# A recurrence in front of an attention kernel: order of the input chunks' normalization, and the refinements of the roots spread over steps

## The chip, the cores and the metric

The kernel runs on one core of a Trainium2 chip, in float32. The metric is the device time of one execution in microseconds (us); less is better. The engines named below are the tensor engine (PE, with its weight loads shown apart as PEld), the vector engine (DVE), the scalar engine (ACT), the general engine (POOL) and the queue engine that issues most transfers (SP). Each engine works through its own instructions in order, and waits on the others by semaphores.

## The reference

A layer of a small sequence model, over x of shape (2, 2048, 256): a plain recurrence with a residual, then a sparse-expert attention with a residual. Both read x through a layer norm.

```python
def _layernorm(x, axis=-1, eps=1e-05):
    m = jnp.mean(x, axis=axis, keepdims=True)
    v = jnp.var(x, axis=axis, keepdims=True)
    return (x - m) / jnp.sqrt(v + eps)
...
xi = jnp.einsum('btd,hd->bth', x, Wi) + bi
def step(h, xt):
    h_new = jnp.tanh(xt + h @ Wh.T + bh)
    return (h_new, h_new)
...
x = L0_attn_x
x = x + _L0_attn_ref(_layernorm(x, axis=-1), Wi, bi, Wh, bh)
x = x + _L0_ffn_ref(_layernorm(x, axis=-1), Wq, Wk, Ws, Wd, Wv, Wo)
```

The attention part has 8 heads of 64, 5 experts of which each token and head takes 2, and is not touched by the change, but for the roots of its own layer norm.

## The kernel before

**Chunks.** Time is cut into 128 segments of 16 steps, for both batches. Chunk c (c = 0 to 15) holds step c of all 128 segments: a tile of 128 partitions by 2 batches by 256. All segments advance together, so one step of the recurrence is one small product for 128 segments.

**Front, pass a (lines 325 to 338).** A loop over k works as a hand-written software pipeline. The order of the calls is the order of the instructions in each engine's queue. In iteration k, it calls in this order:

- turn_in(k-1): four PE transposes of the normalized chunk (line 271), and one DVE copy to SBUF (275);
- project_in(k-2): eight PE matmuls with Wi (283), and two ACT copies with the bias to xi (290);
- step_a(k-3), from k = 5 on: for each batch 8 PE matmuls with Wh (300), a DVE add (308) and an ACT tanh (309);
- norm_in(k): the normalization of chunk k, batch 0 on ACT (248) and batch 1 on POOL (256);
- measure(k+4): for each batch DVE statistics (122) and their aggregate (123). At the last chunk of a group this also makes the group's 1/sqrt(var + eps): three integer and scalar operations (131, 133, 135), then four refinements of three DVE instructions each (141, 143, 145), then the offset -mean times root (152).

The groups of input chunks are IN = [(0, 2), (2, 2), (4, 4), (8, 4), (12, 4)], given as (first chunk, count). Before the loop, measure(0) to measure(3) run, and the bias sum (327). Pass a starts at step 2 and gives the end state of each segment; those ends, moved by one segment, are the starts of pass b.

**Front, pass b (lines 408 to 422).** A second hand-written loop, over k = 0 to 18: step_b(k) runs the step again from the right starts, residual(k-1) turns the state back (four PE transposes, line 347), adds it to x on DVE (348), writes x1 to DRAM from SP's queue (351) and takes the statistics of batch 0 (122, 123). At the last chunk of a group of OUT = [(0, 8), (8, 4), (12, 4)] the roots are computed at once, as above. norm(c) then normalizes chunk c of batch 0 (ACT 379, POOL or DVE 384), and turn(c), an iteration later and only for c below 12, transposes it (392) and copies it (393) into xT, which the attention reads. Chunks 0 and 1 are normalized at k = 9, and so on, two an iteration; chunks 8 to 11 at k = 13 and 14, chunks 12 to 15 at k = 17 and 18. compare() ends the pass: it checks that the end states of both passes agree, else a slow exact version runs at the end (lines 968 and on).

**Attention.** It begins with keys (line 469), queries (486) and experts (511) of the first head on PE; its first keys need xT of chunks 0 to 7 and the PSUM that the front used. Its own layer norm for batch 1 takes the same roots(), with the operations put two per window at windows 21 and on (lines 749 and 866).

**Buffers.** The normalized chunks rotate over three SBUF buffers, the transposes' and the projection's PSUM tiles over two each, the step's PSUM has one per batch.

Of the kernel before, what the change touches and what calls it, by code (L numbers as in the profile page):

```python
# [8 lines left out]
F32 = mybir.dt.float32  # L9
# [5 lines left out]
P = 128  # L15
# [5 lines left out]
def rnn_then_switchhead_kernel(  # L21
# [17 lines left out]
    E, _, DH = Wv.shape  # L39
    H = Wq.shape[1] // DH  # L40
    KC = D // P
    NCH = T // P
# [82 lines left out]
    def roots(pool, var, n, nm):  # L125

        got = {}

        def begin():
            v = pool.tile([P, n], F32, tag="rt_v", name=f"v{nm}")  # L130
            nc.vector.tensor_scalar(v, var, EPS, None, ALU.add)
            half = pool.tile([P, n], I32, tag="rt_i", name=f"i{nm}")
            nc.vector.tensor_scalar(half, v.bitcast(I32), 1, None, ALU.logical_shift_right)
            y = pool.tile([P, n], I32, tag="rt_y", name=f"y{nm}")
            nc.vector.tensor_scalar(y, half, -1.0, float(0x5F3759DF), ALU.mult, ALU.add)
            got["v"], got["y"] = v, y.bitcast(F32)

        def better(k):
            v, y = got["v"], got["y"]
            a = pool.tile([P, n], F32, tag="rt_a", name=f"a{nm}_{k}")  # L140
            nc.vector.scalar_tensor_tensor(a, y, -0.5, y, ALU.mult, ALU.mult)
            h = pool.tile([P, n], F32, tag="rt_h", name=f"h{nm}_{k}")
            nc.vector.tensor_tensor(h, a, v, ALU.mult)
            z = pool.tile([P, n], F32, tag="rt_z" if k < 3 else "rt_r", name=f"z{nm}_{k}")
            nc.vector.scalar_tensor_tensor(z, h, 1.5, y, ALU.add, ALU.mult)
            got["y"] = z

        return got, [begin] + [lambda k=k: better(k) for k in range(4)]

    def offset(dst, mean, root):  # L150

        nc.vector.scalar_tensor_tensor(dst, mean, -1.0, root, ALU.mult, ALU.mult)  # L152
# [53 lines left out]
    TOL = 4 * 2.0**-23  # L206
    S0 = 2
    apart = const.tile([P, 1], F32, name="apart")
    IN = [(0, 2), (2, 2), (4, 4), (8, 4), (12, 4)]
    OUT = [(0, 8), (8, 4), (12, 4)]  # L210
    LATE = 12
    late_of = {}
    with tc.tile_pool(name="prep", bufs=2) as pp, tc.tile_pool(
        name="lna", bufs=2
    ) as lnp, tc.tile_pool(name="step", bufs=2) as sp, tc.tile_pool(
        name="ps_f", bufs=2, space=PSUM
    ) as ps_f, tc.tile_pool(name="ps_h", bufs=1, space=PSUM) as ps_h, tc.manual_schedule():
        group_in = {c: g for g, (c0, n) in enumerate(IN) for c in range(c0, c0 + n)}
        group_out = {c: g for g, (c0, n) in enumerate(OUT) for c in range(c0, c0 + n)}
        norm_of, made, h_of = {}, {}, {}  # L220

        def measure(c):
            g = group_in[c]
            c0, n = IN[g]
            if c == c0:
                norm_of[g] = [lnp.tile([P, 4, B, 2], F32, tag="mv", name=f"mva{g}")]
            mv = norm_of[g][0]
            for b in range(B):
                st = lnp.tile([P, 6], F32, tag="st", name=f"sta{c}_{b}")
                stats((st, mv[:, c - c0, b, :]), xt[c][:, b, :])  # L230
            if c < c0 + n - 1:
                return
            mvf = mv[:, 0:n].rearrange("p j b t -> p (j b) t")
            got, ops = roots(lnp, mvf[:, :, 1], n * B, f"a{g}")
            for f in ops:
                f()
            nb = lnp.tile([P, n * B], F32, tag="nb", name=f"nba{g}")
            offset(nb, mvf[:, :, 0], got["y"])
            norm_of[g] += [got["y"], nb]

        def norm_in(c):
            g = group_in[c]
            _, r, nb = norm_of[g]
            xn = pp.tile([P, B, D], F32, tag="xn", bufs=3, name=f"xn{c}")
            for b in range(B):
                k = (c - IN[g][0]) * B + b
                if b == 0:
                    nc.scalar.activation(
                        xn[:, b, :],
                        xt[c][:, b, :],  # L250
                        AF.Identity,
                        scale=r[:, k : k + 1],
                        bias=nb[:, k : k + 1],
                    )
                else:
                    nc.gpsimd.tensor_scalar(  # L256
                        xn[:, b, :],
                        xt[c][:, b, :],
                        r[:, k : k + 1],
                        nb[:, k : k + 1],  # L260
                        ALU.mult,
                        ALU.add,
                    )
            made[c] = xn

        def turn_in(c):
            xn = made.pop(c)
            tp = ps_f.tile([P, KC, B, P], F32, tag="tp", name=f"tpa{c}")
            for kc in range(KC):
                for b in range(B):  # L270
                    nc.tensor.transpose(
                        tp[:, kc, b, :], xn[:, b, kc * P : (kc + 1) * P], ident
                    )
            xnT = pp.tile([P, KC, B, P], F32, tag="xnT", name=f"xnT{c}")
            nc.vector.tensor_copy(xnT, tp)
            made["T", c] = xnT

        def project_in(c):
            xnT = made.pop(("T", c))
            for mc in range(KC):  # L280
                px = ps_f.tile([P, B, P], F32, tag="px", name=f"px{c}_{mc}")
                for kc in range(KC):
                    nc.tensor.matmul(
                        px.rearrange("p b n -> p (b n)"),
                        lhsT=wi[:, kc, mc * P : (mc + 1) * P],
                        rhs=xnT[:, kc].rearrange("p b n -> p (b n)"),
                        start=kc == 0,
                        stop=kc == KC - 1,
                    )
                nc.scalar.activation(  # L290
                    xi[:, mc, c], px, AF.Identity, bias=bsum[:, mc : mc + 1]
                )
# [27 lines left out]
        def step_b(s):  # L320
            for b in range(B):
                prev = ends[:, :, b, 0:NS] if s == 0 else hs[:, :, s - 1, b, :]
                advance("b", s, b, prev, hs[:, :, s, b, :])

        for c in range(4):
            measure(c)
        nc.vector.tensor_tensor(bsum, bias[:, 0, :], bias[:, 1, :], ALU.add)
        for k in range(NCH + 3):
            if 0 <= k - 1 < NCH:
                turn_in(k - 1)  # L330
            if 0 <= k - 2 < NCH:
                project_in(k - 2)
            if S0 <= k - 3:
                step_a(k - 3)
            if k < NCH:
                norm_in(k)
            if k + 4 < NCH:
                measure(k + 4)

        mv2 = lnp.tile([P, NCH, 2], F32, tag="mv2", bufs=1, name="mv2")  # L340
        root_of = {}

        def residual(c):
            tp = ps_f.tile([P, B, KC, P], F32, tag="tp", name=f"tpb{c}")
            for b in range(B):
                for kc in range(KC):
                    nc.tensor.transpose(tp[:, b, kc, :], hs[:, kc, c, b, :], ident)
            nc.vector.tensor_tensor(
                xt[c], xt[c], tp.rearrange("p b c d -> p b (c d)"), ALU.add
            )  # L350
            nc.sync.dma_start(out=x1d[c], in_=xt[c])
            st = lnp.tile([P, 6], F32, tag="st2", name=f"stb{c}")
            stats((st, mv2[:, c, :]), xt[c][:, 0, :])
            g = group_out[c]
            c0, n = OUT[g]
            if c < c0 + n - 1:
                return
            m = mv2[:, c0 : c0 + n, :]
            got, ops = roots(lnp, m[:, :, 1], n, f"b{g}")
            for f in ops:  # L360
                f()
            nb = lnp.tile([P, n], F32, tag="nb2", name=f"nbb{g}")
            offset(nb, m[:, :, 0], got["y"])
            root_of[g] = (got["y"], nb)

        def norm(c):
            g = group_out[c]
# [39 lines left out]

        jobs = {}
        for c in range(NCH):
            k = 9 + c // 2 if c < 8 else max(OUT[group_out[c]][0] + OUT[group_out[c]][1] + 1, 9 + c // 2)  # L410
            k += (c % 2) if c >= 12 else 0
            jobs.setdefault(k, []).append((norm, c))
            if c < LATE:
                jobs.setdefault(k + 1, []).append((turn, c))
        for k in range(max(jobs) + 1):
            if k < S:
                step_b(k)
            if 1 <= k <= S:
                residual(k - 1)
            for f, c in jobs.get(k, []):  # L420
                f(c)
# [481 lines left out]
    with tc.manual_schedule():  # L903
# [7 lines left out]
        b, n = heads[units[last][0]][0], units[last][1]  # L911
        NW = NT // RUN
        for W in range(NW + LAG):
# [20 lines left out]
            for t in old:  # L934
                if t // HC == last:
                    c = t % HC
# [32 lines left out]
    with tc.If(flag > 0):  # L969
        with tc.tile_pool(name="fr", bufs=1) as fr, tc.tile_pool(  # L970
            name="f2", bufs=2
# [86 lines left out]
            for k in range(2):  # L1058
                for b in range(B):
                    new_logits(b, k)  # L1060
                    for c in range(k * HN, (k + 1) * HN):
# [14 lines left out]
                        got, ops = roots(f2, mv[:, :, 1], 1, f"fb{b}_{c}")  # L1076
# [36 lines left out]
        with tc.tile_pool(name="rows", bufs=1) as rows, tc.tile_pool(  # L1113
            name="row2", bufs=2
        ) as row2, tc.tile_pool(name="ps_a", bufs=1, space=PSUM) as ps_a, tc.tile_pool(
            name="ps_b", bufs=2, space=PSUM
# [150 lines left out]
```

## Time and profile before

| what | us |
|---|---|
| median of 3 runs | 1447.45 (1447.43 to 1448.62) |
| the profiled execution's own time | 1448.96 |
| its span, first to last instruction | 1447.2 |

The span by stages, from the start of one to the start of the next (PE instructions' starts), with the busy time of the engines in it:

| stage | from, to | length | PE | DVE | ACT | mean granted PE clock |
|---|---|---|---|---|---|---|
| pass a, until the transposes of k = 6 | 0 to 33.06 | 33.06 | 12.88 | 21.99 | 8.71 | 1.00 |
| pass a, k = 6 to 15 | 33.06 to 89.95 | 56.89 | 41.69 | 26.38 | 22.80 | 1.00 |
| pass a, k = 16 to 18 | 89.95 to 99.94 | 9.99 | 9.74 | 2.90 | 3.91 | 1.00 |
| pass b, steps 0 to 8 | 99.94 to 121.00 | 21.06 | 20.91 | 15.84 | 7.51 | 1.00 |
| pass b, steps 9 and 10 | 121.00 to 130.85 | 9.85 | 6.79 | 7.15 | 2.50 | 0.83 |
| pass b, steps 11 and 12 | 130.85 to 136.28 | 5.43 | 5.43 | 3.65 | 3.45 | 1.00 |
| pass b, step 13 | 136.28 to 141.82 | 5.54 | 2.83 | 4.85 | 1.92 | 1.00 |
| pass b, steps 14, 15 and its end | 141.82 to 149.05 | 7.23 | 6.19 | 5.85 | 4.55 | 1.00 |
| attention | 149.05 to 1447.20 | 1298.15 | | | | 0.73 to 1.00 |

PE is busy for 1340.4 us of the span (93%), DVE for 1141.6, POOL for 1009.5 and ACT for 705.0. A matmul's end is modelled in this profile, so starts are read rather than ends. An idle time in brackets behind a line of the timeline is that of the engine just ahead of the instruction, with what released it.

### The profile page before, as it was taken

Reading aid. Unit: us, or ns where it says so; the run is one execution under the profiler, and the core shown is the slowest. Engines: PE = TensorE matmul, PEld = TensorE weight load, DVE = VectorE, ACT = ScalarE, POOL = GpSimd, SP = SyncE. Lnnn points to the kernel's source line nnn. Section 1 sums busy time; section 2 is a strip of 40 time slices with the busy share of each in tenths; the row PEclk is TensorE's granted clock in tenths of the full one; section 3 lists DMA queues with packets and bytes.
Section 4 is the critical chain, followed back from the end, with each engine's and each line's share of the span. In section 5 each row is a group of like instructions: output and inputs, shape, how many; then the busy total and the mean of one; then the engine's idle time right before and its main releaser. Section 6 shows DMA issues by size and latency. Waiting matters only on the chain.

```text
span 1447.2 us, 36443 instructions
## 1 busy us (share of the span) xinstructions
PE 1340.4 (93%) x15450; PEld 635.1 (44%) x15450; DVE 1141.6 (79%) x2131; ACT 705.0 (49%) x911; POOL 1009.5 (70%) x590
## 2 busy tenths in 40 slices
PE   4788779999989999989999999999999999999986
PEld 3678324444334444433344455444444444444444
DVE  6537668989887687889988877888888888888752
ACT  2433325555445555544455444555555555555451
POOL 1100038888878768768888866888888888888960
PEclk9999979999999999999999999999999999999999
DMA  6002115657665666556667556566666666766643
GB/s 189 1 9 87 66 45 136 176 149 156 129 144 129 151 147 148 132 103 145 132 139 174 134 136 152 140 139 145 141 145 139 139 143 137 157 139 146 140 106 102
DMA packets 66314, 186.99 MB, mean 129 GB/s; under 512 B 8928, under 2 KB 26464, under 8 KB 66144
## 3 DMA queue, kind: packets, MB, share of 16 engines
q0 software_dynamic: 25056, 97.53, 36.4%
q1 hardware_dynamic: 39456, 86.46, 18.8%
q8 instruction: 123, 2.02, 0.5%
q10 hardware_dynamic: 1632, 0.61, 0.2%
q14 instruction: 47, 0.39, 0.1%
HBM read 59.79 MB, written 50.33 MB: 76 GB/s over the span
## 4 chain that ended last, share of the span: by engine, by line
PE 58%; issue 15%; DVE 11%; POOL 3%; ACT 1%; DVEq 0%; POOLq 0%; ACTq 0%
PE o L629 28%; PE s L570 12%; DVE p L586 7%; PE pq L486 4%; PE pk L469 4%; PE pz L806 3%; PE pv L511 2%; PE pc L648 2%; PE pc L661 1%; PE pl L597 1%; POOL es L613 1%; POOL es L609 1%; POOL es L619 1%; PE py L790 1%; DVE gates L200 0%
## 5 line engine op out<-in xcount | busy, mean ns | idle before, releaser
L586 DVE TENSOR_SCALAR_CACHE_REDUCE p<-s 128x1024 f32<-128x1024 f32 x512 | 596.4, 1221 | 114.2 <-PE s L570 112.1
L602 ACT ACTIVATE p<-p,low 128x1024 f32<-128x1024 f32 x512 | 546.1, 1140 | 55.3 <-DVE low L599 54.9
L570 PE MATMUL s<-q,k 64*32 64x512 f32 x4096 | 482.6, 603 | 13.7 <-DVE p L586 10.4
L570 PE MATMUL s<-qs,k 64*32 64x512 f32 x4096 | 482.6, 603 | 11.1 <-DVE p L586 5.9
L629 PE MATMUL o<-p,v 128*64 128x256 f32 x4096 | 472.5, 383 | 0.0
L609 POOL TENSOR_TENSOR es<-p,p 128x1024 f32<-128x1024 f32 x126 | 329.3, 2613 | 164.9 <-ACT p L602 164.9
L629 PEld LDWEIGHTS o<-p,v 128*64 128x64 f32 x4096 | 282.7, 137 | 194.7 <-ACT p L602 48.6
L613 POOL TENSOR_TENSOR es<-es,p 128x1024 f32<-128x1024 f32 x126 | 299.9, 2380 | 9.9
L640 ACT COPY os<-o 128x256 f32<-128x256 f32 x64 | 23.8, 372 | 394.2 <-PE o L629 394.2
L570 PEld LDWEIGHTS s<-qs,k 64*32 64x32 f32 x4096 | 120.8, 107 | 147.7 <-issue 75.6
L570 PEld LDWEIGHTS s<-q,k 64*32 64x32 f32 x4096 | 120.7, 107 | 147.0 <-issue 67.6
L619 POOL TENSOR_TENSOR es<-es,es 128x1024 f32<-128x1024 f32 x63 | 151.4, 2403 | 4.0 <-DMA es<-p 3.9
L615 POOL DMA_DIRECT2D es<-p x126 | 109.9, 873 | 19.1 <-POOL es L613 14.9
L555 DVE TENSOR_TENSOR pr<-xq,pw 128x1280 f32<-128x1280 f32 x60 | 89.3, 1488 | 31.3 <-ACT pw L539 31.3
L704 DVE TENSOR_TENSOR pro<-pc,mr 128x1280 f32<-128x1280 f32 (+1 forms) x65 | 95.6, 1471 | 2.2
L560 DVE TENSOR_REDUCE v<-pr 128x256 f32<-128x1280 f32 x64 | 94.9, 1486 | 2.1
L620 POOL TENSOR_TENSOR es<-es 128x512 f32<-128x512 f32 x63 | 85.5, 1357 | 4.9
L469 PE MATMUL pk<-xT,wk 128*32 128x512 f32 x512 | 62.2, 604 | 2.5 <-ACT xT L393 1.0
L486 PE MATMUL pq<-xT,wq 128*32 128x512 f32 x512 | 62.2, 603 | 1.4
L720 POOL DMA_DIRECT2D yd<-pro x48 | 56.6, 1180 | 0.8 <-DVE p L586 0.8
L256 POOL TENSOR_SCALAR xn<-x,za,nba 128x256 f32<-128x256 f32 x16 | 8.7, 554 | 64.2 <-DVE nba L152 45.6
L384 POOL TENSOR_SCALAR xn<-x,zb,nbb 128x256 f32<-128x256 f32 x6 | 3.3, 555 | 64.6 <-DVE nbb L152 60.8
(141 smaller groups left out, 1030.3 us busy)
## 6 DMA issues: line engine op xcount, KB each, us to landing
es<-p POOLq DMA_DIRECT2D x126, 512.0 KB, 4.8
xq<-xvd SPq DMA_DIRECT2D x60, 640.0 KB, 3.9
yd<-pro POOLq DMA_DIRECT2D x48, 640.0 KB, 8.2
qs<-q SPq DMA_DIRECT2D x64, 128.0 KB, 2.3
xvd<-xw SPq DMA_DIRECT2D x8, 640.0 KB, 3.3
yd<-pro SPq DMA_DIRECT2D x8, 640.0 KB, 4.0
y<-yd SPq DMA_DIRECT2D x8, 640.0 KB, 5.1
x<-in_x SPq DMA_DIRECT2D x16, 256.0 KB, 5.2
```

The source lines that it names most:

```text
L469: nc.tensor.matmul(pk[g * R : (g + 1) * R], lhsT=wk[:, kc, d0 : d0 + R], rhs=xc[:, kc, c0 // 2 : (c0 + HC) // 2, o, :], start=kc == 0, sto ...
L486: nc.tensor.matmul(pq[g * R : (g + 1) * R, :], lhsT=wq[:, kc, d0 : d0 + R], rhs=xT_of[b][:, kc, n * QB : (n + 1) * QB], start=kc == 0, sto ...
L560: nc.vector.tensor_reduce(v_of[i][:, 4 * part : 4 * part + 4, :], pr, AX.X, ALU.add)
L570: nc.tensor.matmul(ss[g * R : (g + 1) * R, o, :], lhsT=k_of[i][half, c, g * R : (g + 1) * R], rhs=q_of[i, n][o][half, :], start=True, stop ...
L586: nc.vector.tensor_scalar(p, ss, 1.0, None, ALU.mult, ALU.min, accum_out=part_of[u][:, c : c + 1])
L602: nc.scalar.activation(ring[t], ring[t], AF.Exp, scale=-1.0, bias=low_of[t // HC])
L609: nc.gpsimd.tensor_tensor(e, ring[t], ring[t - 1], ALU.add)
L613: nc.gpsimd.tensor_tensor(e, e, ring[t], ALU.add)
L615: nc.gpsimd.dma_start(out=es_of[u, half], in_=ring[t], accum_op=ALU.add)
L619: nc.gpsimd.tensor_tensor(e, e, es_of.pop((u, 1)), ALU.add)
L629: nc.tensor.matmul(o_of[u][g * DH : (g + 1) * DH, :], lhsT=v_of[i][:, 2 * c + o, :], rhs=ring[t][:, o, g * QH : (g + 1) * QH], start=c == ...
L704: nc.vector.tensor_tensor(o_of["p", u][:, s0:s1], po[:, s0:s1].unsqueeze(2).to_broadcast([P, w, E, 2, DH]), o_of["m", u][:, s0:s1].unsquee ...
```

## The change

The edits are four. First, the first chunk is a group of its own (IN begins (0, 1), (1, 3)), and the calls ahead of the loop are interleaved: measure(0), norm_in(0), measure(1), measure(2), turn_in(0), measure(3), the bias sum, norm_in(1), project_in(0); the loop starts at k = 2. Second, norm_in(k) stands at the head of iteration k rather than behind step_a. In iterations 2 and 3 two chunks are measured each, from iteration 4 on one (k+4), as before. Third, every root takes three refinements rather than four. Fourth, in pass b the operations of a root go, for the first two groups of OUT, into a list of which two are issued per iteration behind step_b (a refinement, or the three starting instructions, or the offset, is one operation); norm() of chunks 0 to 7 starts at k = 11, chunks 8 to 11 are all normalized at 15, chunks 12 to 15 at 16 and 17. The last group's root is still computed at once.

```diff
--- before.py
+++ after.py
@@ -141,11 +141,11 @@
             nc.vector.scalar_tensor_tensor(a, y, -0.5, y, ALU.mult, ALU.mult)
             h = pool.tile([P, n], F32, tag="rt_h", name=f"h{nm}_{k}")
             nc.vector.tensor_tensor(h, a, v, ALU.mult)
-            z = pool.tile([P, n], F32, tag="rt_z" if k < 3 else "rt_r", name=f"z{nm}_{k}")
+            z = pool.tile([P, n], F32, tag="rt_z" if k < 2 else "rt_r", name=f"z{nm}_{k}")
             nc.vector.scalar_tensor_tensor(z, h, 1.5, y, ALU.add, ALU.mult)
             got["y"] = z
 
-        return got, [begin] + [lambda k=k: better(k) for k in range(4)]
+        return got, [begin] + [lambda k=k: better(k) for k in range(3)]
 
     def offset(dst, mean, root):
 
@@ -206,7 +206,7 @@
     TOL = 4 * 2.0**-23
     S0 = 2
     apart = const.tile([P, 1], F32, name="apart")
-    IN = [(0, 2), (2, 2), (4, 4), (8, 4), (12, 4)]
+    IN = [(0, 1), (1, 3), (4, 4), (8, 4), (12, 4)]
     OUT = [(0, 8), (8, 4), (12, 4)]
     LATE = 12
     late_of = {}
@@ -322,23 +322,31 @@
                 prev = ends[:, :, b, 0:NS] if s == 0 else hs[:, :, s - 1, b, :]
                 advance("b", s, b, prev, hs[:, :, s, b, :])
 
-        for c in range(4):
-            measure(c)
+        measure(0)
+        norm_in(0)
+        measure(1)
+        measure(2)
+        turn_in(0)
+        measure(3)
         nc.vector.tensor_tensor(bsum, bias[:, 0, :], bias[:, 1, :], ALU.add)
-        for k in range(NCH + 3):
-            if 0 <= k - 1 < NCH:
+        norm_in(1)
+        project_in(0)
+        for k in range(2, NCH + 3):
+            if k < NCH:
+                norm_in(k)
+            if k - 1 < NCH:
                 turn_in(k - 1)
-            if 0 <= k - 2 < NCH:
+            if 0 < k - 2 < NCH:
                 project_in(k - 2)
             if S0 <= k - 3:
                 step_a(k - 3)
-            if k < NCH:
-                norm_in(k)
-            if k + 4 < NCH:
-                measure(k + 4)
+            for c in range(2 * k, 2 * k + 2) if k < 4 else [k + 4]:
+                if c < NCH:
+                    measure(c)
 
         mv2 = lnp.tile([P, NCH, 2], F32, tag="mv2", bufs=1, name="mv2")
         root_of = {}
+        spread = []
 
         def residual(c):
             tp = ps_f.tile([P, B, KC, P], F32, tag="tp", name=f"tpb{c}")
@@ -357,11 +365,18 @@
                 return
             m = mv2[:, c0 : c0 + n, :]
             got, ops = roots(lnp, m[:, :, 1], n, f"b{g}")
-            for f in ops:
-                f()
-            nb = lnp.tile([P, n], F32, tag="nb2", name=f"nbb{g}")
-            offset(nb, m[:, :, 0], got["y"])
-            root_of[g] = (got["y"], nb)
+
+            def end():
+                nb = lnp.tile([P, n], F32, tag="nb2", name=f"nbb{g}")
+                offset(nb, m[:, :, 0], got["y"])
+                root_of[g] = (got["y"], nb)
+
+            ops = ops + [end]
+            if g == len(OUT) - 1:
+                for f in ops:
+                    f()
+            else:
+                spread.extend(ops)
 
         def norm(c):
             g = group_out[c]
@@ -407,7 +422,8 @@
 
         jobs = {}
         for c in range(NCH):
-            k = 9 + c // 2 if c < 8 else max(OUT[group_out[c]][0] + OUT[group_out[c]][1] + 1, 9 + c // 2)
+            c0, n = OUT[group_out[c]]
+            k = 11 + c // 2 if c < 8 else 15 + (c >= LATE)
             k += (c % 2) if c >= 12 else 0
             jobs.setdefault(k, []).append((norm, c))
             if c < LATE:
@@ -415,6 +431,9 @@
         for k in range(max(jobs) + 1):
             if k < S:
                 step_b(k)
+            for f in spread[:2]:
+                f()
+            del spread[:2]
             if 1 <= k <= S:
                 residual(k - 1)
             for f, c in jobs.get(k, []):
```

## The prediction

> **What bounds the kernel now.** I read the table of stages first, then the waits of each stage in front of the attention, then the timeline of one iteration. The attention is 1298 us of the span, but almost none of the edits is in it; what the change can move is the first 149 us. Pass a, iterations 6 to 15, is the largest piece (columns: stretch, length, busy us of PE, PEld, DVE, ACT, POOL with counts, PE clock, DMA share, GB/s; below it, from the waits of 33 to 95 us, total us, times, longest):
>
> ```profile
> 33.06:89.95 56.89, 41.69 (x280) 37.73 (x281) 26.38 (x86) 22.80 (x50) 4.36 (x8) 1.00 0.00 1
> ```
> ```profile
> PEld tpa L271 <- ACT xn L248: 19.2, 11, 2.1
> PE tpa L271 <- ACT xn L248: 16.9, 11, 1.7
> ```
>
> PE, the busiest engine, idles 56.89 − 41.69 = 15.2 us there, and one wait holds it all: the transposes wait for ACT's normalization. The timeline of one iteration says why (start, duration, engine, line):
>
> ```profile
> 78.58 0.66 PE L271 MATMUL tpa<-ident,xn 128*128 128x128 f32 x4 [1.52 <-ACT xn L248]
> ...
> 80.80 1.95 PE L300 MATMUL pha<-ha,wh 128*128 128x128 f32 x16
> ...
> 83.30 0.42 ACT L309 ACTIVATE ha<-prea 128x256 f32<-128x256 f32 x1 [0.48 <-DVE prea L308]
> 83.63 0.58 ACT L248 ACTIVATE xn<-x,nba,za 128x256 f32<-128x256 f32 x1
> 84.26 0.42 PEld L271 LDWEIGHTS tpa<-ident,xn 128*128 128x128 f32 x4 [1.71 <-ACT xn L248]
> ...
> 89.95 0.65 PE L271 MATMUL tpa<-ident,xn 128*128 128x128 f32 x4 [1.52 <-ACT xn L248]
> 90.44 1.89 PE L283 MATMUL px<-xnT,wi 128*128 128x256 f32 x8
> ...
> 92.17 1.95 PE L300 MATMUL pha<-ha,wh 128*128 128x128 f32 x16
> ...
> 93.96 1.89 PE L283 MATMUL px<-xnT,wi 128*128 128x256 f32 x8
> ```
>
> The normalization stands in ACT's queue behind both tanh of the step (83.30), though it needs neither; PE's next transposes wait for it. So the iterations come every (89.95 − 33.06)/10 = 5.69 us. Where no transposes follow (93.96), PE goes straight from step to projection: PE's own pace is 0.49 (transposes to projection) + 1.73 (to the step) + 1.79 (to what follows) = 4.01 us.
>
> In pass b, PE waits where a root is computed in one piece on DVE:
>
> ```profile
> 125.55 0.17 DVE L152 SCALAR_TENSOR_TENSOR nbb<-mv,zb 128x8 f32<-128x8 f32 x1
> 125.63 0.75 DVE L308 TENSOR_TENSOR preb<-phb,xi 128x256 f32<-128x256 f32 x2
> ...
> 126.08 0.75 ACT L309 ACTIVATE hs<-preb 128x256 f32<-128x256 f32 x2 [4.53 <-DVE preb L308]
> ...
> 126.55 3.01 PE L300 MATMUL phb<-hs,wh 128*128 128x128 f32 x16 [3.06 <-ACT hs L309]
> ```
>
> The step's add is queued behind sixteen small instructions (122.45 to 125.63), so tanh and PE stand still; steps 9 and 10 take 9.85 us where two others take 4.68.
>
> **The start of pass a.** The first root waits today for four statistics and 16 small instructions: offset at 10.03, the first transposes at 10.97.
>
> ```profile
> 10.03 0.16 DVE L152 SCALAR_TENSOR_TENSOR nba<-mva,za 128x4 f32<-128x4 f32 x1
> ...
> 10.97 1.94 PE L271 MATMUL tpa<-ident,xn 128*128 128x128 f32 x8 [10.97 <-POOL xn L256]
> ```
>
> Now I go down DVE's queue with these prices: a chunk's measure 1.08 us (10.11 to 11.19), a small root instruction 0.20 (7.06 to 10.03 for 15), the copy 0.57, offset to transposes 0.94. Chunk 0 begins at 4.37 and ends at 5.5; twelve small instructions bring its offset to 7.94, its transposes to 8.9. Two measures end at 10.18, the copy at 10.75, the third measure and its root put the offset at 14.35, the bias sum follows, and chunk 1's transposes start at 15.3, at the slow pace of this stage (0.97 for four) done at 16.3. Copy, two measures, copy and two measures end at 21.8, the root's offset comes at 24.3, chunk 4's transposes at 25.35 (+1.05, as 70.36 to 71.4 for a group of eight). The x transfers cost nothing here: issued 0.75 us apart from 0.76 on, and landing within 6.0 us at most, chunk 3 is in SBUF before 10.75. Iteration 5 has no step matmuls, so iteration 6 begins 0.49 + 1.73 later, at 27.6 instead of 33.06: **5.5 us less** (bounds 3 and 6.5: the interleaved ACT waits all paid, or the projections at full pace at once).
>
> **Normalization at the head.** Normalization k is now issued an iteration before its transposes. Per iteration of 4.01 us, ACT has 0.58 + 2×0.47 + 2×0.42 = 2.36 us, DVE 0.57 + 2×0.37 + 1.08 = 2.4, POOL 0.55: all fit under PE. Taking the offsets of the iteration at 89.95: tanh at +3.83 and +4.73, normalization from +5.06, done +5.7, used at +8.0; step at +2.22 needs a tanh done at +1.1. So ten iterations cost 40.1 instead of 56.9: **16.8 less**. For a hand-over between PE and others that no row shows at this pace I set bounds: none, or 0.2 us for each of three PE groups (4.6 us, 10.8 less).
>
> What gets worse: the root at the end of iterations 7 and 11. Today its 16 instructions lie in PE's wait (44.37 to 50.06 is 5.69 us, as any other). With the waiting gone, 13 instructions follow the measures (+5.7) and put the offset at +8.2; behind it in ACT's queue wait the normalization, both copies to xi and two tanh, and PE's transposes start at +9.25, where PE is ready at +8.02: **1.2 us lost twice, 2.4** (0 to 4; DVE's late copy is needed only by the projection behind those transposes). Pass a from 89.95 is PE-bound already and stays. Sum for pass a: 5.5 + 16.8 − 2.4 = **19.9** (bounds 10 to 23).
>
> **Pass b.** DVE's own chain per step, without waits, is 2.02 us (106.52 to 108.17, plus 0.37), in a period of 21.06/9 = 2.34. Six small instructions (1.2 us) make 3.22 in steps 9 and 10. Step 11 gets one, lost in the 0.3 us of slack. Where chunks are also turned, the period is (136.28 − 130.96)/2 = 2.66; step 12 keeps it, steps 13 and 14 lie between 3.22 and 2.66 + 1.2 = 3.86, and I take the middle, 3.54. From step 15 to the keys it was 149.05 − 144.58 = 4.47; now ACT has two normalizations (0.6 each) in that step, and chunks 8 to 11 are turned behind the last residual: their PSUM comes free with ACT's copies, and the queue of copies adds 1.1 (0 to 2.2): 5.6. New length: 21.06 + 6.44 + 2.34 + 2.66 + 7.08 + 5.6 = 45.2 against 49.1: **4 us less** (1.5 to 5.7). The last root, in one piece still, delays neither: keys, queries and experts occupy PE until 158.1, today too.
>
> A row bears on the clock: after PE's 3.06 us of idling, the 16 matmuls from 126.55 take 3.01 us (2.05 otherwise), four transposes 1.06 (0.60), and the mean clock of 121 to 130.85 is 0.83; after the 2.71 us ahead of 141.82 they take 2.05. The Trainium skill (TensorE: Matmul & The Clock Gate, Part 1: The HAM clock gate) says that some 3.4 us of idling halve PE's clock, until as long a time of activity restores it. The trace agrees roughly, with the start of the slow stretch at 3.06 by its records. By the rule the new waits, about 1 us each, keep the clock and the sum stands; if each of the four lengthened steps were nevertheless slowed as at 126.55 (0.96 + 0.46 + 0.32 us), 7 us would be lost.
>
> **Three refinements.** In the attention the root sheds three small instructions, 0.6 us of DVE in one window in which PE sets the pace: nothing, hidden by PE (0.6 without it).
>
> **Sum.** 19.9 + 4.0 = 23.9 off the span of 1447.2 gives 1423.3; the profiled execution would take 1448.96 − 23.9 = 1425.1. That one lies 1.5 above the median of the runs shown (1447.45), so the median should be **1423.6**, and I say 1424.
>
> **Rivals.**
>
> - *Hand-overs bound pass a* (0.15). For: PE's pace of 4.01 is stitched from the one iteration with no transposes behind it. Against: ACT and DVE have 40% of slack. With 4.6 us an iteration: 10.8 instead of 16.8, the time 1430.
> - *The attention's start gives some back* (0.10). At 172.7 and 199.8 PE idles for 9.69 and 7.34 us behind DVE's gates, and then runs slow: 32 expert matmuls take 12.98 us where 16 take 5.64, so 1.7 more; 48 score matmuls from 207.45 at 0.85 per eight instead of 0.43, 2.5 more. These stretches may last longer or shorter when the start moves: up to 5 either way, the time 1419 to 1429. The same section of the Trainium skill calls the window free-running, which would allow it.
> - *The reordering doesn't bite* (0.05): if the order in ACT's queue were unchanged in effect, by a buffer held too long, only the start and pass b gain, 9.5: 1438. Three buffers for the normalized chunk, each free an iteration before it is refilled, speak against.
> - *Slower* (0.03): PE, dense now, is throttled in the front. It has some 94 us of work in 33 to 149 us; at a granted clock c it pays 94×(1/c − 1), which eats 23.6 at c = 0.80. At the 0.56 seen from 180 to 190 us it is 74, and the time 1498. Against: 0.56 came behind idling, and 95 to 125 us, with PE 28.1 of 30 busy, shows 1.00.
>
> **How the numbers follow.** The forecast has 0.67. Its own range, the large bounds not all at once, is 1419 to 1429. To leave out no more than 2 in 10 I add the hand-over rival with its margin: 1419 to 1432. A measurement of this kernel tells 0.2%, 2.9 us, from no change. Faster holds all but the throttle (0.03) and a small piece of the third rival in which pass b also gives nothing (0.02): 0.95, 0.02 and 0.03.
>
> **What would show it.** In pass a, transposes 4.0 us apart, with no wait for the normalization except behind the roots of iterations 7 and 11 (some 1.2 us there); transposes of iteration 6 near 27.6; pass b's first step near 80; steps 9, 10, 13, 14 of 3.2 to 3.6 us without a stall of PE over 1.5 us; the first keys near 125. I am wrong if the transposes stay over 4.6 us apart, if a wait for PSUM or for the late copies appears in their place, or if the attention's length departs from 1298 us by more than 3.

## The result and the profile after

| | before | changed |
|---|---|---|
| median, same chip | 1448.03 (1447.43 to 1450.22, 4 runs) | 1426.33 (1424.15 to 1428.32, 4 runs) |
| ratio, 95% interval | | 0.9847 (0.9828 to 0.9866) |
| profiled execution, its span | 1448.96, 1447.2 | 1424.15, 1422.3 |

The change makes the kernel 1.5% faster. The span shrinks by 24.9 us, all but 0.2 of it in front of the attention. The stages, with what the prediction said of each:

| stage | before | predicted | after |
|---|---|---|---|
| start of pass a, until the transposes of iteration 6 | 33.06 | 27.6 | 27.58 |
| iterations 6 to 15 | 56.89 | 42.5 | 42.08 |
| iterations 16 to 18 | 9.99 | 9.99 | 9.94 |
| pass b, until the first keys | 49.11 | 45.2 | 44.74 |
| attention | 1298.15 | 1298.15 | 1297.96 |

The same stretches of the changed kernel (length, busy us of PE, PEld, DVE, ACT, POOL with counts, PE clock, DMA share, GB/s); pass b is cut ahead of steps 9 and 13:

```profile
0.00:27.58 27.58, 14.64 (x53) 11.11 (x54) 20.03 (x88) 7.42 (x14) 5.20 (x19) 1.00 0.85 248
27.58:69.66 42.08, 40.03 (x281) 37.55 (x280) 24.63 (x81) 21.64 (x52) 4.32 (x8) 1.00 0.00 1
69.66:79.60 9.94, 9.69 (x71) 8.89 (x69) 3.33 (x8) 4.57 (x11) 0.00 (x0) 1.00 0.00 1
79.60:100.66 21.06, 20.91 (x177) 19.77 (x177) 15.83 (x40) 7.50 (x18) 0.00 (x0) 1.00 0.24 87
100.66:112.28 11.62, 9.96 (x84) 9.49 (x85) 9.94 (x35) 3.80 (x10) 1.63 (x3) 1.00 0.26 93
112.28:124.34 12.06, 10.62 (x86) 9.15 (x84) 10.62 (x39) 8.41 (x24) 1.65 (x3) 1.00 0.30 109
```

In iterations 6 to 15, PE is busy for 40.03 of 42.08 us. Its idle time is down from 15.2 us to 2.05, and the table of PE's waits in pass a, from 27.5 us on, has one line left, with the two waits behind the roots of iterations 7 and 11 (total, times, longest):

```profile
PE tpa L271 <- ACT xn L248: 2.0, 2, 1.0
```

The timeline of pass a shows both kinds of iteration:

```profile
31.53 0.60 PE L271 MATMUL tpa<-ident,xn 128*128 128x128 f32 x4
31.96 1.89 PE L283 MATMUL px<-xnT,wi 128*128 128x256 f32 x8
33.69 1.95 PE L300 MATMUL pha<-ha,wh 128*128 128x128 f32 x16
35.48 0.60 PE L271 MATMUL tpa<-ident,xn 128*128 128x128 f32 x4
...
39.71 0.17 DVE L152 SCALAR_TENSOR_TENSOR nba<-mva,za 128x8 f32<-128x8 f32 x1
39.80 0.68 DVE L275 COPY xnT<-tpa 128x512 f32<-128x512 f32 x1
39.96 0.60 ACT L248 ACTIVATE xn<-x,nba,za 128x256 f32<-128x256 f32 x1 [3.35 <-DVE nba L152]
...
40.62 0.70 PE L271 MATMUL tpa<-ident,xn 128*128 128x128 f32 x4 [1.03 <-ACT xn L248]
```

From 31.53 to 35.48 is 3.95 us, without a wait. At a root, ACT sits for 3.35 us on the offset (39.71) with two copies and two tanh queued behind the normalization, and the next transposes come 5.14 us after the last: 1.19 more than 3.95. In pass b the two lengthened steps show as short waits with the clock kept, where one stall of 3.06 us and slow matmuls stood:

```profile
102.98 1.96 PE L300 MATMUL phb<-hs,wh 128*128 128x128 f32 x16
104.78 0.60 PE L355 MATMUL tpb<-ident,hs 128*128 128x128 f32 x4
106.44 2.05 PE L300 MATMUL phb<-hs,wh 128*128 128x128 f32 x16 [1.07 <-ACT hs L309]
108.33 0.60 PE L355 MATMUL tpb<-ident,hs 128*128 128x128 f32 x4
109.52 2.05 PE L300 MATMUL phb<-hs,wh 128*128 128x128 f32 x16 [0.59 <-ACT hs L309]
```

And the end of pass b, where the keys wait for the last copy of the turned chunks:

```profile
122.36 0.44 PE L407 MATMUL tpc<-ident,xn 128*128 128x128 f32 x2 [0.22 <-ACT xn L394]
123.20 0.63 PE L407 MATMUL tpc<-ident,xn 128*128 128x128 f32 x4 [0.40 <-ACT xT L408]
124.34 0.64 PE L488 MATMUL pk<-xT,wk 128*32 128x512 f32 x4 [0.52 <-ACT xT L408]
```

One thing does not fit: the span shrank by 24.9 us, the median by 21.7. Three of the four executions of the changed kernel are slower than the profiled one, by up to 4.2 us.

### The profile page after: what moved, and what is told of

It is laid out like the page before. It is cut to its first block, busy times and chain, and to the rows that moved or that the text cites. A ratio compares the mean times of both kernels' runs of the same rounds, so it can differ in the third digit from the quotient of the medians.

```text
span 1422.3 us, 36420 instructions
## 1 busy us (share of the span) xinstructions
PE 1339.2 (94%) x15450; PEld 634.3 (45%) x15450; DVE 1135.1 (80%) x2104; ACT 703.0 (49%) x911; POOL 1009.3 (71%) x590
## 4 chain that ended last, share of the span: by engine, by line
PE 58%; issue 15%; DVE 11%; POOL 4%; ACT 1%; DMA 1%; DVEq 0%; POOLq 0%; ACTq 0%
PE o L648 28%; PE s L589 12%; DVE p L605 7%; PE pq L505 4%; PE pk L488 4%; PE pz L825 3%; PE pv L530 3%; PE pc L667 2%; PE pc L680 1%; POOL es L632 1%; POOL es L628 1%; POOL es L638 1%; PE pl L616 1%; PE py L809 1%; DMA es<-p 1%
## 5 line engine op out<-in xcount | busy, mean ns | idle before, releaser
L634 POOL DMA_DIRECT2D es<-p x126 | 110.0, 873 | 19.1 <-POOL es L632 15.2
L571 POOL TENSOR_TENSOR pr<-xw,gates 128x1280 f32<-128x1280 f32 x4 | 11.0, 2775 | 52.2 <-DVE gates L201 52.2
L530 PE MATMUL pv<-wvg,xT 128*128 128x400 f32 x128 | 47.6, 522 | 0.0
```

Source lines behind the costliest of these rows:

```text
L634: nc.gpsimd.dma_start(out=es_of[u, half], in_=ring[t], accum_op=ALU.add)
```

## The experiments

**The head of the iteration alone.** In the kernel before, only the normalization is moved.

```diff
         for k in range(NCH + 3):
+            if k < NCH:
+                norm_in(k)
...
-            if k < NCH:
-                norm_in(k)
```

> The kernel before, with the normalization of chunk k moved to the head of iteration k and nothing else. If ACT's order alone makes PE wait in pass a: transposes some 3.95 us apart from iteration 6 on, but for the two iterations behind a root, which now has 16 small instructions and costs 1.2 + 0.6 = 1.8 us each time; iteration 6 begins near 31 (33.06 before), pass b near 82 to 84, the first keys' matmul near 133 (149.05 before), so some 16 us less, median near 1432. Rival, that the earlier roots at the start and the three refinements are needed for the shorter iterations: transposes over 4.6 us apart, the first keys later than 138.

Measured: 1433.49 against 1448.12, ratio 0.9887 (0.9866 to 0.9909); the first keys at 132.24. Transposes are 3.95 to 4.06 us apart, but 5.74 and 5.75 at the roots, which have four refinements here. From iteration 6 (at 31.45) to pass b (84.79) it takes 53.34 us against 66.88 before: 13.5 less, where 16.8 for ten iterations less twice 1.8 makes 13.2. Unforeseen was a second gain: the same stall of pass b as before is followed by matmuls at full pace here.

```profile
107.74 0.60 PE L347 MATMUL tpb<-ident,hs 128*128 128x128 f32 x4
111.40 2.05 PE L300 MATMUL phb<-hs,wh 128*128 128x128 f32 x16 [3.06 <-ACT hs L309]
113.29 0.60 PE L347 MATMUL tpb<-ident,hs 128*128 128x128 f32 x4
```

**The head undone.** The opposite: in the changed kernel, the normalization stands behind step_a again.

```diff
         for k in range(2, NCH + 3):
-            if k < NCH:
-                norm_in(k)
...
                 step_a(k - 3)
+            if k < NCH:
+                norm_in(k)
```

> The changed kernel with the normalization behind the step again, everything else of the change kept. If the order is the cause: transposes 5.69 us apart again, iteration 6 near 29.4 (27.58 in the changed kernel), pass b near 96 (79.60), first keys near 141 (124.34), so 16 to 17 us more, median near 1443. Rival, that DVE's shorter work (groups, refinements) had shortened the iterations: transposes clearly under 5.69 us apart, and less than 10 us more.

Measured: 1440.12, ratio 0.9945 (0.9929 to 0.9962); iteration 6 at 30.57, pass b at 97.46, the keys at 142.23. Iterations 6 to 18 take 66.89 us, as long as before. The wait that the change removed is back in PE's waits from 30 to 97 us:

```profile
PE tpa L271 <- ACT xn L248: 16.9, 11, 1.7
```

So the place in ACT's queue alone holds this part; neither the start nor the spread roots shorten it. Iteration 6 comes 1.2 us later than expected, because PE lost clock in the start (0.69 from 25.05 to 30.57 us, behind 2.90 us of idling; more on this below).

**Pass b's roots in one piece.** The changed kernel with the operations issued at once and norm() at its old iterations.

```diff
-            if g == len(OUT) - 1:
-                for f in ops:
-                    f()
-            else:
-                spread.extend(ops)
+            for f in ops:
+                f()
...
-            k = 11 + c // 2 if c < 8 else 15 + (c >= LATE)
+            k = 9 + c // 2 if c < 8 else max(c0 + n + 1, 9 + c // 2)
```

> The changed kernel with each root of pass b computed in one piece, and the chunks normalized and turned in the iterations of before; three refinements. If the stall behind DVE's queue is what the spreading removes: pass a as in the changed kernel (pass b begins at 79.6), two stalls of PE of some 2.5 us in pass b; 0.6 us shorter each than before, so if the clock of PE stays full behind them the pass is 1.5 us longer than in the changed kernel, and if it halves as before 3.2 us longer: first keys at 125.8 to 127.5. Rival, that spreading only moves the wait to the pass's end: first keys within 0.7 us of 124.34.

Measured: 1428.39, ratio 0.9862 (0.9846 to 0.9879), which overlaps with that of the changed kernel. The stage tells more: pass b takes 47.80 us (80.84 to 128.64) instead of 44.74, so spreading is worth 3.1. Of this, some 1.7 is clock, lost behind the first stall:

```profile
103.80 0.60 PE L355 MATMUL tpb<-ident,hs 128*128 128x128 f32 x4
106.86 3.29 PE L300 MATMUL phb<-hs,wh 128*128 128x128 f32 x16 [2.46 <-ACT hs L309]
109.94 1.04 PE L355 MATMUL tpb<-ident,hs 128*128 128x128 f32 x4
```

The sixteen matmuls took 3.29 instead of 2.05, the transposes 1.04 instead of 0.60.

**Four refinements** in the changed kernel.

```diff
-        return got, [begin] + [lambda k=k: better(k) for k in range(3)]
+        return got, [begin] + [lambda k=k: better(k) for k in range(4)]
```

> The changed kernel with four refinements. Three more small instructions of 0.2 us per root: if all of them lie on the path, 0.6 us for each of the three roots before iteration 6 (27.58 becomes 29.4), 0.6 for each of the two later ones of pass a, and 0.5 for each of the two spread ones of pass b: 4.1 us in all, first keys near 128.4. Rival, that DVE has slack for them except ahead of the first transposes: 0.6 to 1.8 us, first keys under 126.2.

Measured: 1430.45 (1425.65 to 1430.85), ratio 0.9877 (0.9861 to 0.9894). In the profile, which is of the fastest of the four executions, the keys come 3.38 us later than in the changed kernel: iteration 6 at 29.33 (1.75 more, its clock undisturbed), each root iteration 5.74 instead of 5.14, pass b 45.16 (0.42 more). Expected were 4.1 in all.

**The changed kernel again,** to see where its executions differ.

> The changed kernel once more, on the chip of the next three. Its own runs lay between 1424.2 and 1428.3. If the scatter is PE's clock, runs with a lower mean clock are the longer ones, by about 1.7 us for each 3.4 us more at half clock (1422.3 us of span at 0.985 against 1426.6 at 0.980), and the profile shows the front as before: first keys at 124.3 to 125.6. Rival, that something in the front varies: then the first keys move with the run's time.

Measured: 1425.5 (1424.12 to 1427.92), ratio 0.985 (0.9835 to 0.9865); all eight executions of it have the median 1425.8. The longer ones have the lower mean granted clock, as expected: from 0.985 at 1424.1 us to 0.980 at 1428.3. Its profile shows something else in the start, in front of iteration 6:

```profile
24.96 1.11 PE L271 MATMUL tpa<-ident,xn 128*128 128x128 f32 x4 [3.57 <-ACT xn L248]
25.86 3.10 PE L283 MATMUL px<-xnT,wi 128*128 128x256 f32 x8
28.80 0.38 PE L271 MATMUL tpa<-ident,xn 128*128 128x128 f32 x2
```

and the first profile, at the same place:

```profile
25.35 0.66 PE L271 MATMUL tpa<-ident,xn 128*128 128x128 f32 x4 [2.60 <-ACT xn L248]
25.85 1.89 PE L283 MATMUL px<-xnT,wi 128*128 128x256 f32 x8
27.58 0.60 PE L271 MATMUL tpa<-ident,xn 128*128 128x128 f32 x4
```

PE has finished the work of chunks 1 to 3 here and waits for the root of chunks 4 to 7. In the second execution it had come to full pace earlier (at 15.18 us instead of 20.42), so it ran out of work earlier, idled for 3.57 us, and then ran slowly: the transposes take 1.11 instead of 0.66, the projection 3.10 instead of 1.89. The clock of 24.9 to 28.8 us is 0.57 there, and 1.00 in the first:

```profile
24.90:28.80 3.90, 3.84 (x13) 3.27 (x14) 2.55 (x9) 1.69 (x5) 1.71 (x4) 0.57 0.01 4
```

Iteration 6 starts at 28.80 instead of 27.58, and the keys at 125.57. Yet the second execution takes no longer than the first (1424.12 and 1424.15 us): its attention is 1.1 us shorter. So the first keys moved, and the time did not follow.

All six profiles of kernels with the changed start in which PE idled for 3.57 or 3.58 us at this place lost clock behind it, and their iteration 6 came at 28.6 to 29.3. Shorter waits there went either way: behind 2.51, 2.60 and 2.63 us the clock was kept, behind 2.81 and 2.90 it was lost (0.65 and 0.69). In the experiment with the head alone it was lost behind 2.08 us, with 0.58 from 27.65 to 31.45:

```profile
27.65 0.66 PE L271 MATMUL tpa<-ident,xn 128*128 128x128 f32 x4 [2.08 <-ACT xn L248]
28.14 3.52 PE L283 MATMUL px<-xnT,wi 128*128 128x256 f32 x8
```

**Measuring a chunk more ahead,** so that the roots of iterations 7 and 11 are ready an iteration earlier.

```diff
-            for c in range(2 * k, 2 * k + 2) if k < 4 else [k + 4]:
+            for c in range(2 * k, 2 * k + 2) if k < 5 else [k + 5]:
```

> The changed kernel with chunks 9 and on measured one iteration earlier, so that the roots of the third and fourth group lie in iterations 6 and 10 and their offsets are there an iteration before the normalization that needs them. If the 1.2 us behind each root is ACT's queue standing still for the offset: all transposes from iteration 6 on 3.95 to 4.1 us apart, pass b at 77.2 (79.6), 2.4 us less. Rival, that DVE's 2.6 us of root hold PE by another way, the late add of the step: 5.1 us once more, one iteration earlier, and nothing is gained.

Measured: 1423.52, ratio 0.983 (0.9816 to 0.9843). Pass b starts at 78.75, 0.85 earlier; expected were 2.4. ACT's wait is gone from PE's waits, another one stands there twice, in gaps of 4.79 us:

```profile
PE px L283 <- DVE xnT L275: 1.2, 2, 0.6
```

Now the transposes are on time, and the copy behind the root in DVE's queue is late for the projection. The root in one piece blocks one queue or the other.

**Earlier turns at the end of pass b.** The second root gets three operations at k = 13, chunks 8 and 9 turn one iteration sooner, and chunks 12 to 15 start at 16 as in the changed kernel.

```diff
-            k = 11 + c // 2 if c < 8 else 15 + (c >= LATE)
+            k = 11 + c // 2 if c < 8 else 14 + c // 10 if c < LATE else 16
...
-            for f in spread[:2]:
+            w = 3 if k == 13 else 2
+            for f in spread[:w]:
```

> The changed kernel with three operations of the second spread root in iteration 13, so that chunks 8 and 9 are normalized at 14 and turned at 15, chunks 10 and 11 at 15 and 16. If the four turns behind the last residual, each waiting for ACT's copies out of two PSUM buffers, are what lengthens the end of pass b (6.40 us from step 15 to the first keys, 4.47 before the change): two turns less there, 0.8 to 1.2 us less, first keys near 123.3; three more small instructions in iteration 13 cost up to 0.6 of it. Rival, that the end is set by the last step's tanh and residual: no gain, first keys at 124.3 or later.

Measured: 1428.05, ratio 0.9855 (0.984 to 0.987); pass b takes 44.94 us instead of 44.74. No gain: what the end saves (5.99 instead of 6.40 from step 15 to the keys) the step ahead pays (3.60 instead of 3.00).

**PE kept busy in the attention's first waits.** Matmuls that nobody reads stand in PE's queue ahead of the two waits of the second rival: 30 and 20 of them, then 18 and 13.

```diff
+    def keep_busy(n, nm):
+        spare = ps_o.tile([P, QH], F32, tag="o", name=nm)
+        for _ in range(n):
+            nc.tensor.matmul(spare, lhsT=ident, rhs=wq[:, 0, 0:QH], start=True, stop=True)
+
+    at(two, 1, keep_busy, 20, "spare1")
...
+                if t == 7:
+                    keep_busy(30, "spare0")
```

> The changed kernel with 30 and 20 matmuls of 128x256 whose result nobody reads, put where PE waits for DVE's gates at the start of the attention (9.7 and 7.3 us of idling). If PE's clock behind these waits is what the attention's start pays: the two stretches of 10.2 us at half clock shrink or vanish, the 32 expert matmuls take 11.3 us instead of 12.7, the scores behind the second wait 0.43 us per eight instead of 0.85, and the attention is 3 to 5 us shorter; the runs scatter less. Rival, that DVE sets the pace there: the clock is full and the time within 1 us; or the added matmuls outlast the wait and it grows.

> The changed kernel with 18 and 13 unread matmuls in the two waits instead of 30 and 20: one took 0.44 us, so 7.9 and 5.7 us, inside waits of 9.7 and 7.3. If the clock behind the waits is a cost of the attention's start: both stretches at half clock gone, the matmuls end before the gates, the 32 expert matmuls take 11.0 us (12.7), the attention is 2.5 to 3.5 us shorter at the same later half-clock stretches, median near 1423. Rival, that DVE sets the pace behind both waits: within 1 us of the changed kernel.

Measured with 30 and 20: 1426.27, ratio 0.9849 (0.9836 to 0.9863): nothing. The clock of the two stretches was 1.00, but the 30 took 13.22 us, 0.44 each, and outlasted the wait of 9.7 they were to fill, so the size hid the answer. With 18 and 13: 1422.75, ratio 0.9817 (0.9802 to 0.9831), the attention 1295.3 us instead of 1297.96 and 1296.83 in the two profiles of the changed kernel (ten profiles without spare matmuls there lie between 1295.1 and 1302.1, so its first part says more than the whole). The changed kernel there, behind its wait:

```profile
158.27 1.06 PE L589 MATMUL s<-q,k 64*32 64x512 f32 x1 [9.69 <-DVE p L605]
...
160.17 12.67 PE L530 MATMUL pv<-wvg,xT 128*128 128x400 f32 x32
```

and with 18 and 13 spare matmuls (each is recorded as two):

```profile
151.15 8.04 PE L925 MATMUL spare<-wq,ident 128*128 128x256 f32 x36
160.96 0.61 PE L589 MATMUL s<-q,k 64*32 64x512 f32 x1 [1.77 <-DVE p L605]
...
162.10 11.01 PE L530 MATMUL pv<-wvg,xT 128*128 128x400 f32 x32
```

The 32 expert matmuls lose 1.66 us to the clock in the changed kernel, close to the 1.7 of the rival's rows. Behind the second wait the scores run at 0.43 us per eight instead of 0.85, but PE then waits for DVE's reductions (line 605), and only 0.8 of the rival's 2.5 us is won. From the first keys to the first matmul of line 648 it takes 62.85 us instead of 65.99, 3.1 us less. So the first wait costs what the rival said and the second costs less. Both stand in the kernel before and in the changed one (9.69 and 7.34 us of idling in each).

**Pass a's roots spread as well,** and then with the spare matmuls too. The last operation of a root, end(), makes the offset.

```diff
...
+            ops = ops + [end]
+            if g < 3:
+                for f in ops:
+                    f()
+            else:
+                spread_in.extend(ops)
...
-            for c in range(2 * k, 2 * k + 2) if k < 4 else [k + 4]:
+            for c in range(2 * k, 2 * k + 2) if k < 6 else [k + 6]:
...
+            w = {6: 3, 7: 2, 10: 3, 11: 2}.get(k, 0)
+            for f in spread_in[:w]:
+                f()
+            del spread_in[:w]
```

> The changed kernel with the roots of the third and fourth input group spread too: chunks 8 to 11 measured two per iteration in 4 and 5, and on two iterations ahead of before; three operations of the root in iteration 6 (10), two in 7 (11). If all that these roots still cost is DVE's 2.6 us in one piece, by ACT's wait for the offset or, without it, by the late copy ahead of a projection (0.84 us twice in the run with earlier measures): transposes from iteration 6 on 3.95 to 4.1 us apart throughout, pass b 2.2 to 2.4 us earlier, at 77.2 or, with the other start of PE's clock, 78.5. Rival, that DVE has not the room beside the statistics: gaps of over 4.4 us remain.

> Both of these edits at once on the changed kernel. If they act in different stages they add: 2.3 us in pass a and 2.5 to 3.5 in the attention's start, 5 us less than the changed kernel, median near 1421. Rival, that an earlier pass a or the kept clock moves a half-clock stretch elsewhere: less than 3 us.

Measured: 1421.62, ratio 0.9813 (0.9796 to 0.9829), and with both 1418.77 (1417.2 to 1421.99), ratio 0.9801 (0.9782 to 0.9819). In both profiles all transposes from iteration 6 on are 3.95 us apart, and PE has no wait from 30 us to pass b. With the roots spread, iteration 6 to pass b takes 49.44 us instead of 52.02. Against the median of 1425.8 of the changed kernel, in part from another chip, the two edits alone give 4.2 and 3.1, together 7.0. Of the 4.2, the stage shows 2.6; where the rest comes from is not shown.

**The start's wait filled too.** Five unread matmuls ahead of chunk 4's transposes.

```diff
+            if k == 5:
+                spare = ps_h.tile([P, KC, NS], F32, tag="ph0", name="spare_a")
+                for _ in range(5):
+                    nc.tensor.matmul(
+                        spare.rearrange("p c n -> p (c n)"), lhsT=ident, rhs=wi[:, 0, :], start=True, stop=True
+                    )
```

> The kernel with both edits (roots of pass a spread, 18 and 13 unread matmuls in the attention's start), and five unread matmuls of 128x256 (2.2 us at the full clock) ahead of chunk 4's transposes, where PE waits 2.6 us in one profile of the changed kernel and 3.6 in the others. If the spread of the start, iteration 6 at 27.6 in the one and 28.8 to 29.3 in the others, is PE's clock halved behind that wait: no half-clock stretch before pass b, iteration 6 near 27.3 to 27.6, pass b at 76.9 to 77.2 (78.0 and 78.3 without), runs 1 us shorter and closer together, median near 1418. Rival, that the start's clock depends on when PE first got busy alone: the stretch stays, pass b near 78.

Measured: 1416.71 (1416.31 to 1417.83) against 1449.14, ratio 0.9773 (0.976 to 0.9786). Its start:

```profile
21.32 2.32 PE L349 MATMUL spare_a<-wi,ident 128*128 128x256 f32 x10
25.05 0.66 PE L280 MATMUL tpa<-ident,xn 128*128 128x128 f32 x4 [1.42 <-ACT xn L257]
25.55 1.89 PE L292 MATMUL px<-xnT,wi 128*128 128x256 f32 x8
27.27 0.60 PE L280 MATMUL tpa<-ident,xn 128*128 128x128 f32 x4
```

PE reached full pace early here too, as in the second profile of the changed kernel, but with the wait cut from 3.57 to 1.42 us the matmuls stay at full pace (1.89), and iteration 6 starts at 27.27, pass b at 76.76. The five executions lie within 1.5 us of each other, where the eight of the changed kernel spread over 4.2.

## Why the prediction was right, and where it was off

**The normalization at the head, 16.8 less: right.** Measured 3.95 us from transposes to transposes, against 4.01 as PE's own pace. The two experiments that do or undo this edit alone show 13.5 us (with the dearer roots in it) and the whole of the old 66.9 us back. The rival of dear hand-overs falls, and so does that of a reordering without effect.

**The roots of iterations 7 and 11, 1.2 lost twice: right.** Measured 1.19 at the first; iterations 6 to 15 took 42.08 against a predicted 42.5. The working by ACT's queue was right as far as it went; had that queue been freed, DVE's late copy would have held PE for 0.6, as the experiment with earlier measures showed. The prediction had named this copy as needed only by the projection behind those transposes.

**The start, 5.5 less: right in one execution, 1.2 too much in others.** This is the step that was mis-sized. The prediction walked down DVE's queue and met the first profile to 0.02 us, but it gave the wait of PE in the start no cost. There is a new one of 2.6 to 3.6 us ahead of chunk 4's transposes, and the prediction's sentence that the new waits are about 1 us and keep the clock overlooked it. Where it is 3.57, the clock was 0.57 behind it, 1.2 us were lost until iteration 6 in the second profile, and up to 1.7 in a profile of a kernel with the same start. Of the nine profiles with this start as it is in the changed kernel, two have iteration 6 at 27.58 and seven at 28.58 to 29.30. So the close match is in part luck: the profiled execution was one of the two.

That filling the wait keeps the clock is shown by the last experiment, which differs from the one before it by that edit alone: iteration 6 starts at 27.27 instead of 28.59, the keys at 121.52 instead of 122.79, and the median is 2.1 lower (the intervals of the two ratios just touch). In the changed kernel itself the edit was not tried alone.

**The scatter of the executions stays open.** That the start makes it is not shown, and two things speak against it. The second profile of the changed kernel has the slow start and is as fast as the first. And the kernel with 30 and 20 spare matmuls, which lost clock in the start too, has executions within 1.8 us. The time goes with the mean clock of the whole execution, but no trace shows where the changed kernel's slow executions lose it. Two profiles with a mean clock of 0.981, those of the head alone and of the earlier turns, have an attention longer by some 4 us (1301.7 and 1302.1) than the changed kernel's first profile, with a lower clock from 1320 us on (0.97 to 1380 us and 0.93 behind, where the first profile of the changed kernel has 1.00 and 0.96). A third profile at 0.981, with the roots in one piece, does not (1298.6).

**Pass b, 4.0 less: right in sum (4.37), with two sizes off.** The steps lengthened by a root take 3.46 and 3.08 us where 3.22 twice was said, but they are the ones one later, since the operations stand behind a step and hold up the next. The second pair was dearer in the prediction (3.54 twice) than measured: one step of 3.00, the others at 2.66 and 2.76. The end, from step 15 to the keys, took 6.40 instead of 5.6, so it grew by 1.9, not 1.1, within the stated bounds. The prediction put this growth down to the queue of ACT's copies. The profiles show PE busy for 5.13 us of the end, with the transposes moved there, against 3.43 before, so 1.7 of the 1.9 us is PE's own busy time and 0.2 is more waiting. What ACT's copies cost by themselves is not shown; with two of the turns moved a step ahead the end shrank by only 0.4. That the sum fits is in part luck: steps 13 and 14 were put 1.4 too long, the end 0.8 too short.

**Spread against the clock.** Part of what spreading is worth is the clock. PE was slowed behind an idle of 2.46 us by its records in the experiment with the roots in one piece, behind 3.06 in the kernel before, and behind 2.08 in the start with the head alone, yet not behind 2.60 in the start of the changed kernel, nor behind the same 3.06 in the experiment with the head alone. So the length of the wait alone doesn't decide. The Trainium skill (TensorE: Matmul & The Clock Gate, Part 1: The HAM clock gate) calls the window of about 3.4 us free-running; waits of one length with different outcomes agree with that. The threshold of one idle window that the same section gives is not what the records of 2.08 and 2.46 us show.

**Three refinements, nothing in the attention: right.** With four it took 1296.1 us, no more than with three, though 0.6 us could not be told in the range of 1295.1 to 1302.1 that the profiles without spare matmuls show. In front they are worth 3.4 us (the experiment with four), which the prediction had inside the terms of the start, the roots and pass b.

**The rival of the attention's start** gave no shift of note in the changed kernel: 1297.96 and 1296.83 against 1298.15. In other experiments the attention took from 1295.1 us (the head undone) to 1302.1 (the earlier turns), so shifts of the size that the rival priced do occur, and that none came here is luck as far as the record shows. **The throttle** in the dense front fell: the clock is 1.00 from 27.58 to the keys in the first profile.

**The sum** of 23.9 stands against 24.9 in the profiled execution (1424.15, predicted 1425.1). The median is 2.7 above the predicted 1423.6, and the step from one execution to the median failed: the changed kernel's profiled execution was the fastest of its four, while that of the kernel before was above its median.

## What to carry to other kernels

In a queue worked in order, put what another engine needs next ahead of what itself waits: here one move of two lines was worth some 14 us (14.6 done alone, 14.3 undone alone). A chain of small instructions is spread over several steps, and its cost is looked for in every queue behind it (ACT's first, DVE's next), since taking it out of one showed the other. When a stage shrinks, ask where the bounding engine now waits for over 2 us: it can pay for that wait a second time in clock, and unread matmuls in the wait, shorter than it, took that back here where PE set the pace behind it (in the start and at the attention's first wait), and little of it where DVE did (at the second).

## What the runs showed of the hardware that was not expected

PE's slow stretch depends on more than the wait ahead of it: 2.08 and 2.46 us of idling brought it, 2.60 did not, and 3.06 did both. Unread matmuls of 128x256 in float32 cost 0.44 us each at full pace, 13.22 us for 30, so that filling a wait needs them counted. The transposes follow the clock, 0.60 to 0.66 us for four at full and 1.04 to 1.11 at the low one. And small differences ahead decide the clock later: PE at full pace 5 us earlier in the start ran into a wait longer by 1.0 us (3.57 instead of 2.60) and came out later. In the first 20 us the clock of the profile can't be used for this: it reads 1.00 there, also in the changed kernel from 15.0 to 20.4 us, where eight projection matmuls take 3.35 us instead of 1.89.
